# Two masked-attention layers: one count per group, and projections in halves in the counts' bank

## The chip, the cores and the metric

One core of one Trainium2 chip runs the whole program. The metric is the device time of one launch in microseconds; three runs of the kernel before gave a median of 3095.62 (3095.62 to 3095.9).

## The reference

There are 16 graphs ("batches") of N = 1024 nodes with E = 256 features, in float32, and a 0/1 adjacency matrix of 1024 x 1024 for each. Each batch goes through two layers. A layer normalizes the features of each node, applies a relu, projects to queries, keys and values, computes attention scores only where the adjacency says so, and adds the projected result to its input.

```python
for layer, (H, D) in enumerate([(4, 64), (8, 32)]):
    h = maximum(layernorm(x), 0)
    q, k, v = h @ Wq, h @ Wk, h @ Wv            # layer 1 has biases
    s = q @ k.T / sqrt(D)                       # per head: 1024 x 1024
    s = where(adj > 0, s, -inf)
    x = x + softmax(s) @ v @ Wo + bo
```

The softmax divides each head's weighted sum of values by the sum of its exponentials. That sum of exponentials over the keys is what this kernel calls a count.

## The kernel before

**Tiling.** For each batch and layer the queries are split into two halves of 512 (`qh`), and the heads into two groups (`g`) that fill 128 partitions: 2 heads of 64 in layer 0, 4 heads of 32 in layer 1. So a layer of a batch has four groups; in the order (qh, g) they are called group 0 to group 3 here. A group is made of steps: 4 in layer 0, 8 in layer 1. In a step, `scores` (L493) computes four blocks of 128 keys x 512 queries on TensorE into two pairs of PSUM banks; `exponentials` (L508) masks each pair on VectorE (L524) into a tile `p` in SBUF and applies the exponential on ScalarE (L530); `weigh` (L535) multiplies the result with the values on TensorE (L542), two steps behind the scores. Layer 0 of batch b + 2 and layer 1 of batch b + 1 follow layer 1 of batch b, so that a batch's two layers never run back to back: the list of 768 steps is L0 of batch 0, then L0 of batch b + 1 and L1 of batch b by turns. One turn is 16 steps of layer 0 (run two at a time) and 32 steps of layer 1.

**PSUM.** Six of the eight banks are three pairs (`ps_s`) used in a ring by the scores, and by projections, transposes and output products in between. The two other banks (`ps_o`) hold one tile each: `po` for the weighted values and `pz` for the counts.

**SBUF ring of the exponentials.** The tile of an even step is one of 7 (`p0`); an odd step takes two half tiles, each one of 2 (`p10`, `p11`). So the odd tile of step s is written again by step s + 4, once its reader on GpSimd (POOL) is through.

**Counting in layer 1.** A count is a matmul of `p` with ones (`count`, L381): TensorE sums over 128 keys. To need few of them, tiles are added first. `count_steps` (L645) does it: behind each odd step, POOL adds the odd step's two half tiles into the even step's tile (L659, two instructions). Four such pairs make a group. Pairs are then joined by a DMA that adds one tile to another (`accumulate`, L642, issued on POOL, 1 MiB each): in groups 0 to 2 the first pair into the second, and the third into the fourth. So two tiles are left, each counted by 4 matmuls of 512 columns (each of which the hardware runs as two) or, in two following steps, by halves of 256 columns (`halves`, L689). In group 3 the first two and the third are accumulated on, and one tile is counted. The last group of batch 14 (`brief`) and all of layer 1 of batch 15 (`pairs`) count without this chain.

**After a group.** `end_group` (L700) gives the steps in which the count is copied out (`spread`), inverted (`invert`), read back in broadcast form (`fetch`), multiplied into the result on POOL (`normalize`), and, once per query half, multiplied by Wo and added to x (`end_half`, L478, 16 matmuls).

**Inputs of later layers.** While layer 1 of batch b runs, the inputs of layer 0 of batch b + 2 are prepared (`other`), and those of layer 1 of batch b + 1 (`mine` in the next turn of the loop over b): `stats` on VectorE and POOL, `norm` on ScalarE, then transposition by blocks through DRAM (`turn_blocks` on VectorE, `put_blocks` and `place_blocks` by DMAs on SyncE's queue, tile names `hn` and `turned`), then `k`, `q` (8 matmuls of 512 each) and `values` (16 matmuls of 256), each into a pair of PSUM banks, copied out by ScalarE or VectorE.

**Order.** The program writes its order out by hand. `later(i, f, ...)` puts a piece of work into step i; `Stream.run` (L588) emits for each step: scores; then the weighing that is due (in an even step of layer 1 with a piece of `LARGE` work it waits for the odd step that follows); then the counts that are due; then masking and exponentials; then the other pieces, the large ones last. A DMA that POOL issues stands in POOL's own instruction order: if it has to wait, what follows on POOL waits too.

The steps given to the pieces are offsets: `c` is the first step of layer 1 of batch b, and `a` = c - 16 the first step of the layer 0 (of batch b + 1) that stands ahead of it; a - 22 to a - 1 lie in layer 1 of batch b - 1. In `end_group` the offsets count from the step in which a group's last weighing is due, two behind the group's last step.

Of the kernel before, what the change touches and what calls it, by code (L numbers as in the profile page):

```python
# [18 lines left out]
P = 128  # L19
# [4 lines left out]

LARGE = ("k", "q", "values", "end_half")
COUNTS = ("count", "count_added")
# [64 lines left out]
def fast_program(ctx, tc, a, w, loads, chk):  # L91
# [89 lines left out]
    class Inputs:  # L181
# [98 lines left out]
        def place_blocks(self, half):  # L280
# [3 lines left out]
            for k in range(4):  # L284
                nc.sync.dma_start(
                    hT[ts(k, 32)].rearrange("p c (g q) -> p c g q", q=P), blocks[k]
                )

        def kq(self, half, is_q):
            if half == 0 and not is_q:  # L290
                self.kT = actp.tile([P, 2, N], F32, tag="kT", name=f"kT_{self.n}")
                self.v = actp.tile([P, NT, E], F32, tag="v", name=f"v_{self.n}")
            if is_q:
# [31 lines left out]
        def test(self):  # L325

            held = small.tile([P, 32], F32, tag="held", bufs=1, name=f"held_{self.n}")
            for i in range(self.sums.shape[1] // 32):
                for bound, op in ((SUM_MIN, ALU.is_ge), (SUM_MAX, ALU.is_le)):
# [3 lines left out]
                    nc.gpsimd.tensor_mul(chk, chk, held)  # L333

        def k(self, half):
            self.kq(half, False)
# [231 lines left out]
    class Stream:  # L568
# [76 lines left out]
        def count_steps(self, i, st):  # L645
# [7 lines left out]
            elif j % 2:  # L653
# [6 lines left out]
                if gr.pairs and (st.last or gr.hurry):  # L660
                    self.later(i + 2, gr.count, one, j == 1, st.last)
                elif gr.pairs:
                    self.halves(i + 3, gr, one, j == 1, False)
                elif j == 1:
                    gr.one = one
                elif j == 3:
                    self.accumulate(one, gr.one)
                    gr.one = one
                    if not gr.last:
                        self.halves(i + gr.waits[0], gr, one, True, False)  # L670
                    if gr.brief:
                        self.later(i + 6, gr.count, one, True, False)
                elif gr.brief and j == 5:
                    self.halves(i + 5, gr, one, False, False)
                elif gr.brief:
                    self.later(i + 4, gr.count, one, False, st.last)
                elif j == 5:
                    gr.two = one
# [21 lines left out]
        def end_group(self, i, gr):  # L700
# [6 lines left out]
            if gr.layer == 0:  # L707
# [121 lines left out]
    def block_inputs(inp, half, turn, put, place, *at):  # L829

        later(turn, inp.turn_blocks, half)
        later(put, inp.put_blocks, half)
        later(place, inp.place_blocks, half)
        for i, f in zip(at, (inp.k, inp.q, inp.values)):
            later(i, f, half)

# [18 lines left out]
    for b in range(B - 1):  # L855
# [7 lines left out]
        else:  # L863
            norms(mine, 0, a - 20, a - 16, a - 15, a - 13, bias=a)
            block_inputs(mine, 0, a - 10, a - 8, a - 4, a, a + 2, a + 8)
            norms(mine, 1, a - 14, a - 10, a - 8, a - 6, bias=a + 6)
            block_inputs(mine, 1, a, a + 6, a + 7, c, c + (6 if b + 2 < B else 10), c + 2)
        for i, u in zip((0, 2, 4, 6, 7, 9, 11, 13), range(NT)):
            later(a + i, masks[b].second, u)
        if b + 2 < B:  # L870
# [3 lines left out]
            if b == 0:  # L874
                norms(other, 0, a + 12, a + 14, c, c + 1, bias=c + 34)
                block_inputs(other, 0, c + 2, c + 3, c + 4, c + 8, c + 16, c + 18)
                norms(other, 1, c + 3, c + 4, c + 6, c + 7, bias=c + 36)
                block_inputs(other, 1, c + 8, c + 9, c + 12, c + 22, c + 26, c + 30)
# [267 lines left out]
```

## Time and profile before

| | |
|---|---|
| median of 3 runs | 3095.62 us |
| the profiled execution | 3096.61 us, of it 3094.8 from the first to the last instruction |
| granted TensorE clock | 0.999 |
| TensorE matmuls busy | 3074.0 us (99%) |
| VectorE, ScalarE, GpSimd busy | 2474.6 (80%), 2230.1 (72%), 2436.5 (79%) |
| one layer 0 in the middle (batch 7) | 76.8 us |
| one layer 1 in the middle (batch 5) | 113.1 us |

The page gives for each group of instructions its line, engine, operation and tiles, how often it ran, the time it was busy, the mean of one, and how long its engine was idle just before it and for whom. A timeline row gives the start, the time to the end of the last of the merged instructions, and in brackets the idle time before it. A "landing" is the time at which a DMA has signalled that its data is written, counted from its issue.

### The profile page before, as it was taken

Reading aid. Unit: us, or ns where it says so; the run is one execution under the profiler, and the core shown is the slowest. Engines: PE = TensorE matmul, PEld = TensorE weight load, DVE = VectorE, ACT = ScalarE, POOL = GpSimd, SP = SyncE. Lnnn points to the kernel's source line nnn. Section 1 sums busy time; section 2 is a strip of 40 time slices with the busy share of each in tenths; the row PEclk is TensorE's granted clock in tenths of the full one; section 3 lists DMA queues with packets and bytes.
Section 4 is the critical chain, followed back from the end, with each engine's and each line's share of the span. In section 5 each row is a group of like instructions: output and inputs, shape, how many; then the busy total and the mean of one; then the engine's idle time right before and its main releaser. Section 6 shows DMA issues by size and latency. Waiting matters only on the chain.

```text
span 3094.8 us, 47328 instructions
## 1 busy us (share of the span) xinstructions
PE 3074.0 (99%) x17406; PEld 1221.3 (39%) x17406; DVE 2474.6 (80%) x2698; ACT 2230.1 (72%) x2436; POOL 2436.5 (79%) x1554
## 2 busy tenths in 40 slices
PE   9999999999999999999999999999999999999998
PEld 4443433434334343343434334343343433434333
DVE  6778788887888878788787888878788787887777
ACT  5677777777777777778677677776777777776676
POOL 3578878787887878878788787887878778787787
PEclk9999999999999999999999999999999999999999
DMA  5215545454463544635445353554535545453331
GB/s 129 66 58 118 127 106 129 121 112 119 107 137 110 119 118 103 143 108 117 120 103 134 107 127 110 113 127 110 127 110 111 132 105 125 120 112 84 79 77 33
DMA packets 259230, 341.37 MB, mean 110 GB/s; under 512 B 58288, under 2 KB 218288, under 8 KB 241968
## 3 DMA queue, kind: packets, MB, share of 16 engines
q0 software_dynamic: 19152, 139.47, 22.6%
q1 hardware_dynamic: 238368, 197.51, 22.2%
q8 instruction: 138, 2.26, 0.3%
q10 hardware_dynamic: 1472, 1.31, 0.2%
q14 instruction: 100, 0.82, 0.1%
HBM read 149.95 MB, written 47.96 MB: 64 GB/s over the span
## 4 chain that ended last, share of the span: by engine, by line
PE 95%; DVE 2%; POOL 1%; DMA 1%; issue 1%; ACT 0%; SPq 0%; DVEq 0%; ACTq 0%; POOLq 0%
PE ps L501 31%; PE po L542 29%; PE pq L304 15%; PE pv L345 8%; PE py L483 7%; PE pz L387 4%; DVE p L524 1%; POOL p L659 1%; DMA inv<-vd 0%; DMA x<-in_x_dram 0%; SPq L420 0%; ACT p L530 0%; DMA sums<-s 0%; POOL cat L447 0%; DMA adj<-in_adj_dram 0%
## 5 line engine op out<-in xcount | busy, mean ns | idle before, releaser
L524 DVE SCALAR_TENSOR_TENSOR p<-mask,ps 128x1024 f32<-128x1024 fp8e5 x1536 | 1791.9, 1214 | 366.2 <-PE ps L501 348.5
L530 ACT ACTIVATE p<-p 128x1024 f32<-128x1024 f32 x1536 | 1607.0, 1056 | 628.1 <-DVE p L524 572.1
L659 POOL TENSOR_TENSOR p<-p,p 128x1024 f32<-128x1024 f32 x510 | 1212.8, 2430 | 166.3 <-PE po L542 165.8
L501 PE MATMUL ps<-qT,kT 32*128 32x512 f32 (+1 forms) x6144 | 1073.3, 628 | 3.6 <-DVE p L524 3.0
L542 PE MATMUL po<-p,v 128*32 128x512 f32 (+1 forms) x6144 | 980.2, 600 | 0.7 <-ACT cat L399 0.4
L501 PEld LDWEIGHTS ps<-qT,kT 32*128 32x128 f32 (+1 forms) x6144 | 349.7, 184 | 587.9 <-issue 243.1
L542 PEld LDWEIGHTS po<-p,v 128*32 128x32 f32 (+1 forms) x6144 | 234.3, 118 | 680.3 <-issue 474.5
L555 POOL TENSOR_TENSOR p<-p 128x1024 f32<-128x1024 f32 x128 | 302.7, 2365 | 90.5 <-DVE p L554 85.1
L554 POOL TENSOR_TENSOR p<-p,p 128x1024 f32<-128x1024 f32 x64 | 150.8, 2356 | 169.6 <-DVE p L551 126.3
L345 PE MATMUL pv<-wv,hT 128*128 128x256 f32 x1024 | 237.8, 385 | 0.0
L304 PE MATMUL pq<-hT,wk 128*128 128x512 f32 x512 | 236.7, 605 | 0.7 <-DVE p L524 0.6
L304 PE MATMUL pq<-hT,wq 128*128 128x512 f32 x512 | 236.6, 605 | 0.1
L483 PE MATMUL py<-wo,cat 128*128 128x256 f32 x1008 | 234.4, 386 | 0.7 <-DVE p L524 0.6
L447 POOL TENSOR_TENSOR cat<-cat,inv 128x512 f32<-128x512 f32 x127 | 174.9, 1383 | 73.0 <-DMA inv<-vd 72.6
L345 PEld LDWEIGHTS pv<-wv,hT 128*128 128x128 f32 x1024 | 189.4, 190 | 72.1 <-DVE p L524 21.3
L483 PEld LDWEIGHTS py<-wo,cat 128*128 128x128 f32 x1008 | 186.3, 190 | 74.8 <-issue 25.1
L551 DVE TENSOR_TENSOR p<-p 128x1024 f32<-128x1024 f32 x128 | 181.7, 1419 | 0.0
L387 PE MATMUL pz<-p,ones 128*32 128x256 f32 (+1 forms) x1928 | 180.4, 444 | 0.5 <-DMA p<-p 0.5
L643 POOL DMA_DIRECT2D p<-p x133 | 122.6, 922 | 63.7 <-POOL p L659 30.3
L221 ACT ACTIVATE hn<-x,shift,rstd 128x256 f32<-128x256 f32 x251 | 135.6, 588 | 43.7 <-DMA turned<-hn 32.2
L399 ACT COPY cat<-po 128x512 f32<-128x512 f32 x128 | 73.4, 573 | 118.5 <-PE py L483 96.6
L488 DVE TENSOR_TENSOR x<-py,x 128x1024 f32<-128x1024 f32 x63 | 77.1, 1224 | 101.9 <-PE py L483 101.2
(62 smaller groups left out, 1773.1 us busy)
## 6 DMA issues: line engine op xcount, KB each, us to landing
p<-p POOLq DMA_DIRECT2D x133, 1024.0 KB, 7.8
adj<-in_adj_dram SPq DMA_DIRECT2D x504, 128.0 KB, 3.0
turned<-hn SPq DMA_DIRECT2D x58, 512.0 KB, 3.8
hT<-turned SPq DMA_DIRECT2D x232, 128.0 KB, 2.8
x<-in_x_dram SPq DMA_DIRECT2D x128, 128.0 KB, 3.1
inv<-vd SPq DMA_DIRECT2D x128, 128.0 KB, 3.0
inv<-vd SPq DMA_DIRECT2D x252, 64.0 KB, 3.3
out_dram<-x SPq DMA_DIRECT2D x124, 128.0 KB, 2.3
```

Source lines behind the costliest of these rows:

```text
L304: nc.tensor.matmul(pq[:, m, :], wt[self.layer][:, c, ts(m, P)], self.hT[half][:, c, :], start=(c == 0), stop=(c == 1),)
L345: nc.tensor.matmul(pv[:, i, :], self.hT[half][:, c, ts(i, P)], w.v[self.layer][:, c, :], start=(c == 0), stop=(c == 1),)
L387: nc.tensor.matmul(self.s[ts(r, 32), q], w.ones.to_broadcast([P, 32]), of[:, q], start=start and not part, stop=stop and part != 0,)
L447: nc.gpsimd.tensor_mul(o, o, inv)
L483: nc.tensor.matmul(py[:, i, :], self.half.cat[:, c, ts(i, P)], w.o[self.layer][:, c, :], start=(c == 0), stop=(c == 1),)
L501: nc.tensor.matmul(st.ps[i // 2][:, i % 2, :], gr.inp.kT[r * D : (r + 1) * D, gr.g, ts(kt, P)], gr.inp.qT[gr.qh][r * D : (r + 1) * D, gr.g ...
L524: nc.vector.scalar_tensor_tensor(out=half, in0=gr.mask.m[gr.qh][:, kt // 4, :, kt % 4].unsqueeze(1).to_broadcast([P, 2, 512]), scalar=-EDG ...
L530: nc.scalar.activation(half, half, AF.Exp, scale=gr.scale)
L542: nc.tensor.matmul(gr.o[r * D : (r + 1) * D, :], gr.inp.v[:, kt, h * D : (h + 1) * D], st.halves[i // 2][:, i % 2, :], start=(kt == 0), st ...
L551: nc.vector.tensor_add(a, a, b)
L555: nc.gpsimd.tensor_add(a, a, b)
L659: nc.gpsimd.tensor_add(half, half, of)
```

## The change

In layer 1 of batches 0 to 14, groups 0 to 2 now accumulate all four pairs into one tile, which is counted once: the first pair into the second, the second into the third in the same step as that pair's adds, and the third into the fourth two steps behind the adds (`self.later(i + k, self.accumulate, ...)`, k = 2). The count stands 9, 7 and 8 steps behind the end of group 0, 1 and 2, in one piece except in group 1. Group 3 is as it was.

Two thirds of the projections for layer 0 of batches 2 to 15 are made in two parts, each with one half of the output, in the bank `pz` of the counts (`part`, `k_part`, `q_part`, `values_part`), and the parts stand in different steps. Keys: steps c + 8 and c + 10 for half 0, c + 20 and c + 22 for half 1. Queries: c + 12 and c + 16 for half 0. Values: c + 28 and c + 30 for half 1.

Some pieces move: for layer 0's second query half the normalization from 7 to 11 and the product from 11 to 13 steps behind its end (steps c + 12 and c + 14); the copy and inverse of groups 0 and 2 of layer 1; the statistics for the next layer 1 by two or three steps earlier.

```diff
-LARGE = ("k", "q", "values", "end_half")
+LARGE = ("k", "q", "values", "end_half", "k_part", "q_part", "values_part")
...
+        def part(self, half, is_q, m):
+            if m == 0 and is_q:
+                self.qT[half] = actp.tile(
+                    [P, 2, 512], F32, tag="qT", bufs=3, name=f"qT_{self.n}_{half}"
+                )
+            to = self.qT[half] if is_q else self.kT[:, :, ts(half, 512)]
+            wt = w.q if is_q else w.k
+            pq = ps_o.tile([P, 512], F32, tag="pz", name=f"pq_{self.n}_{half}_{int(is_q)}_{m}")
+            for c in range(2):
+                nc.tensor.matmul(
+                    pq, wt[self.layer][:, c, ts(m, P)], self.hT[half][:, c, :],
+                    start=(c == 0), stop=(c == 1),
+                )
+            (nc.vector.tensor_copy if is_q else nc.scalar.copy)(to[:, m, :], pq)
...
+        def values_part(self, half, m):
+            pv = ps_o.tile([P, 512], F32, tag="pz", name=f"pv_{self.n}_{half}_{m}")
+            pv = pv.rearrange("p (t e) -> p t e", e=E)
+            for i in range(2):
+                for c in range(2):
+                    nc.tensor.matmul(
+                        pv[:, i, :], self.hT[half][:, c, ts(2 * m + i, P)],
+                        w.v[self.layer][:, c, :], start=(c == 0), stop=(c == 1),
+                    )
+            nc.scalar.copy(self.v[:, 4 * half + 2 * m : 4 * half + 2 * m + 2, :], pv)
...
-            self.waits = ((5, 5), (7, 7), (7, 6), None)[2 * qh + g]
+            self.waits = (9, 7, 8, 4)[2 * qh + g]
...
-                elif j == 3:
+                elif gr.brief:
+                    if j == 3:
+                        self.accumulate(one, gr.one)
+                        self.later(i + 6, gr.count, one, True, False)
+                    elif j == 5:
+                        self.halves(i + 5, gr, one, False, False)
+                    else:
+                        self.later(i + 4, gr.count, one, False, True)
+                elif gr.last and j == 5:
+                    gr.two = one
+                elif not st.last:
                     self.accumulate(one, gr.one)
                     gr.one = one
-                    if not gr.last:
-                        self.halves(i + gr.waits[0], gr, one, True, False)
...
-                elif not gr.last:
-                    self.accumulate(one, gr.two)
-                    if gr.qh:
-                        self.later(i + 6, gr.count, one, False, True)
+                else:
+                    of, k = (gr.two, 1) if gr.last else (gr.one, 2)
+                    self.later(i + k, self.accumulate, one, of)
+                    if gr.g and not gr.qh:
+                        self.halves(i + gr.waits, gr, one, True, True)
                     else:
-                        self.halves(i + gr.waits[1], gr, one, False, True)
-                else:
-                    self.later(i + 1, self.accumulate, one, gr.two)
-                    self.later(i + 4, gr.count, one, True, True)
+                        self.later(i + gr.waits, gr.count, one, True, True)
...
-                at = (3, 4, 5, 7, 11) if gr.qh else (3, 5, 6, 7, 11)
+                at = (3, 4, 5, 11, 13) if gr.qh else (3, 5, 6, 7, 11)
...
-                at = ((6, 12, 15, 19), (8, 12, 14, 17, 19), (6, 9, 11, 14), None)[2 * gr.qh + gr.g]
+                at = ((9, 13, 15, 19), (8, 12, 14, 17, 19), (8, 11, 13, 15), None)[2 * gr.qh + gr.g]
...
-            norms(mine, 0, a - 20, a - 16, a - 15, a - 13, bias=a)
+            norms(mine, 0, a - 22, a - 18, a - 15, a - 13, bias=a)
...
-            norms(mine, 1, a - 14, a - 10, a - 8, a - 6, bias=a + 6)
+            norms(mine, 1, a - 14, a - 13, a - 8, a - 6, bias=a + 6)
...
-                block_inputs(other, 0, c, c + 1, c + 2, c + 8, c + 16, c + 18)
+                block_inputs(other, 0, c, c + 1, c + 2, (c + 8, c + 10), (c + 12, c + 16), c + 18)
...
-                block_inputs(other, 1, c + 7, c + 8, c + 12, c + 22, c + 26, c + 30)
+                block_inputs(other, 1, c + 7, c + 8, c + 12, (c + 20, c + 22), c + 26, (c + 28, c + 30))
```

More of the change, by code (lines that the diff above doesn't have):

```diff
@@ L287, in place_blocks, with open_kv @@
                 )
+        def open_kv(self):
+            self.kT = actp.tile([P, 2, N], F32, tag="kT", name=f"kT_{self.n}")
+            self.v = actp.tile([P, NT, E], F32, tag="v", name=f"v_{self.n}")
         def kq(self, half, is_q):
             if half == 0 and not is_q:
-                self.kT = actp.tile([P, 2, N], F32, tag="kT", name=f"kT_{self.n}")
-                self.v = actp.tile([P, NT, E], F32, tag="v", name=f"v_{self.n}")
+                self.open_kv()
             if is_q:
@@ L333, in test, with k_part, q_part @@
                     nc.gpsimd.tensor_mul(chk, chk, held)
+        def part(self, half, is_q, m):
[12 more added lines that the diff above has]
+            (nc.vector.tensor_copy if is_q else nc.scalar.copy)(to[:, m, :], pq)
+        def k_part(self, half, m):
+            if half == 0 and m == 0:
+                self.open_kv()
+            self.part(half, False, m)
+        def q_part(self, half, m):
+            self.part(half, True, m)
+        def values_part(self, half, m):
[8 more added lines that the diff above has]
+            nc.scalar.copy(self.v[:, 4 * half + 2 * m : 4 * half + 2 * m + 2, :], pv)
         def k(self, half):
@@ L665, in count_steps @@
                     gr.one = one
-                elif j == 3:
+                elif gr.brief:
[9 more added lines that the diff above has]
+                elif not st.last:
                     self.accumulate(one, gr.one)
                     gr.one = one
-                    if not gr.last:
-                        self.halves(i + gr.waits[0], gr, one, True, False)
[L671 to L678, printed above, removed]
-                elif not gr.last:
-                    self.accumulate(one, gr.two)
-                    if gr.qh:
-                        self.later(i + 6, gr.count, one, False, True)
-                    else:
-                        self.halves(i + gr.waits[1], gr, one, False, True)
-                else:
-                    self.later(i + 1, self.accumulate, one, gr.two)
-                    self.later(i + 4, gr.count, one, True, True)
+                else:
[3 more added lines that the diff above has]
+                        self.halves(i + gr.waits, gr, one, True, True)
+                    else:
+                        self.later(i + gr.waits, gr.count, one, True, True)
         def halves(self, i, gr, one, start, stop):
@@ L833, in block_inputs @@
         later(place, inp.place_blocks, half)
-        for i, f in zip(at, (inp.k, inp.q, inp.values)):
-            later(i, f, half)
+        parts = inp.k_part, inp.q_part, inp.values_part
+        for i, f, part in zip(at, (inp.k, inp.q, inp.values), parts):
+            if type(i) is tuple:
+                for m in range(2):
+                    later(i[m], part, half, m)
+            else:
+                later(i, f, half)
     for i, f, half in (0, inp.k, 1), (0, inp.values, 0), (0, inp.values, 1), (2, inp.q, 1):
@@ L875, in fast_program @@
                 norms(other, 0, a + 12, a + 14, c, c + 1, bias=c + 34)
[L876 removed]
+                block_inputs(other, 0, c + 2, c + 3, c + 4, (c + 8, c + 10), (c + 12, c + 16), c + 18)
                 norms(other, 1, c + 3, c + 4, c + 6, c + 7, bias=c + 36)
[L878 removed]
+                block_inputs(other, 1, c + 8, c + 9, c + 12, (c + 20, c + 22), c + 26, (c + 28, c + 30))
             else:
                 norms(other, 0, a + 10, a + 12, a + 13, a + 15, bias=c + 34)
[L881 removed]
+                block_inputs(other, 0, c, c + 1, c + 2, (c + 8, c + 10), (c + 12, c + 16), c + 18)
                 norms(other, 1, c + 2, c + 4, c + 5, c + 6, bias=c + 36)
[L883 removed]
+                block_inputs(other, 1, c + 7, c + 8, c + 12, (c + 20, c + 22), c + 26, (c + 28, c + 30))
             at = 5, 8, 10, 12, 14, 45, 49, 51, 53
```

## The prediction

> **What bounds the kernel now.** I read the page first, then the groups with shapes kept apart, then the timelines of TensorE and GpSimd in one batch, then the DMA view of two short windows.
>
> ```profile
> PE 3074.0 (99%) x17406; PEld 1221.3 (39%) x17406; DVE 2474.6 (80%) x2698; ACT 2230.1 (72%) x2436; POOL 2436.5 (79%) x1554
> L659 POOL TENSOR_TENSOR p<-p,p 128x1024 f32<-128x1024 f32 x510 | 1212.8, 2430 | 166.3 <-PE po L542 165.8
> L387 PE MATMUL pz<-p,ones 128*32 128x256 f32 (+1 forms) x1928 | 180.4, 444 | 0.5 <-DMA p<-p 0.5
> L643 POOL DMA_DIRECT2D p<-p x133 | 122.6, 922 | 63.7 <-POOL p L659 30.3
> ```
>
> TensorE is idle for 21 us in all, so a matmul taken out pays at once, as long as nobody else becomes late. The candidate is POOL: in layer 1 of batch 5 (span 1149.80 to 1262.90) the windows view has it busy 94.60 of 113.10 us. All times below count from that 1149.80, and step n is the n-th step from there; other batches differ by tenths. Here is POOL from step 18 on:
>
> ```profile
> 1223.28 9.39 POOL L659 TENSOR_TENSOR p<-p,p 128x1024 f32<-128x1024 f32 x4 [1.75 <-PE po L542]
> 1232.96 0.87 POOL L643 DMA_DIRECT2D p<-p  x1 [0.30 <-POOL p L659]
> ...
> 1248.69 4.72 POOL L659 TENSOR_TENSOR p<-p,p 128x1024 f32<-128x1024 f32 x2 [1.64 <-PE po L542]
> 1253.37 1.28 POOL L447 TENSOR_TENSOR cat<-cat,inv 128x512 f32<-128x512 f32 x1
> 1254.62 4.71 POOL L659 TENSOR_TENSOR p<-p,p 128x1024 f32<-128x1024 f32 x2
> 1259.62 0.89 POOL L643 DMA_DIRECT2D p<-p  x1 [0.30 <-POOL p L659]
> 1261.42 4.70 POOL L659 TENSOR_TENSOR p<-p,p 128x1024 f32<-128x1024 f32 x2 [0.90 <-PE po L542]
> 1267.91 0.87 POOL L643 DMA_DIRECT2D p<-p  x1 [1.79 <-PE po L542]
> ```
>
> Two things to see. POOL waits for TensorE before each pair of adds, by 0.4 to 2.2 us: that is all its slack. And the last row: the accumulate at 1267.91 reads the tile that the one of 1259.62 writes. That one lands at 1267.37 (issue plus 7.7), and POOL starts 0.54 later; in all 14 batches with this pair the second starts 0.5 to 0.6 us after the first has landed. So the wait put down to PE is one for the landing, and it stops everything behind it on POOL. Landings depend on company; the DMA view of 1212:1227 and then of 1231:1246:
>
> ```profile
> p<-p POOLq DMA_DIRECT2D x1, 1024.0 KB, 6.9
> ```
>
> ```profile
> p<-p POOLq DMA_DIRECT2D x1, 1024.0 KB, 10.0
> turned<-hn SPq DMA_DIRECT2D x1, 512.0 KB, 9.6
> inv<-vd SPq DMA_DIRECT2D x4, 64.0 KB, 7.5
> ```
>
> At step 22 the accumulate meets the block write and the read-backs: 10.0 to 11.8 us there, median 10.1, in 14 of 14 batches.
>
> **What TensorE saves.** From one start to the next in the trace, a half count (8 matmuls of 256) takes 0.55 us and a full one (8 of 512) 0.98. Before, groups 0 and 1 have four halves each (2.2), group 2 two halves and a full one (2.1). After: 0.98, 1.1, 0.98. That is 1.2 + 1.1 + 1.1 = 3.4 us a batch, in batches 0 to 14: 51 us at most. The projections cost the same in halves: a whole one holds TensorE 3.64 us, a half 1.82. They fill the pairs of steps that lose their counts (10, 14, 20, 28), which matters because a bare pair is 4.0 us on TensorE against 4.86 us of masking on VectorE and 4.7 of adds on POOL; every pair now has at least 5.1.
>
> **What it adds off TensorE.** 45 accumulates (three in groups 0 to 2, not two): 0.3 + 0.61 us of POOL each. Two copies of 512 for one of 1024: ScalarE 2 x 0.586 for 1.005, VectorE 2 x 0.69 for 1.224, four times a batch, some 0.7 us on engines with over 15 us free in that stage. The parts leave the score buffers alone and share the bank of the counts instead; the closest case is the k half of step 22, whose copy (behind that step's exponentials) ends near 83.7 while the count in step 24 starts at 86.6. If that cover went, 1 us per case would show. Layer 0's normalization (two of 1.25) leaves step 8, behind the new second accumulate of group 0, for step 12: POOL reaches step 13's adds at 52.5 for 50.2, and is level again by step 19. SP issues group 0's four read-outs in step 18 instead of 15 and its inverse in 22 instead of 21, with the same block write and read-backs behind them; it waits for others most of the time there, so nothing. ScalarE stands for the block write before the norm of step 24 (2.1 us in this batch); it gets there 2.2 us earlier and the write does not, so the exponentials of step 25 end near 96.4, just when TensorE wants them in step 27: between nothing and 1 us, and I take nothing, because the later event below covers it.
>
> **The wait that is added.** A1, A2 and A3 are a group's accumulates in order. A2 (behind the third pair's adds) reads what A1 wrote one pair of adds before. In groups 0 and 1 a whole product lies between (pair 7.64 us): wait under 1 us. In group 2 it is a half (5.85). I follow the chain from step 19, which TensorE reaches at 71.18 - 2.18 (four half counts gone) + 0.98 (group 0's count, now in step 18) = 69.98, plus 0.2 since layer 0's products in step 14 now come right behind their normalization on POOL (moved to step 12, behind group 0's A3).
> - Adds start 2.3 behind the step (as in the trace): 72.5; 4.69; statistics moved here from step 22, 1.58; A3 of group 1 at 79.1; adds from 79.7; A1 of group 2 at 84.7.
> - It lands 10.1 later (write and read-backs stand at the same place), 94.8. POOL is through with its adds at 90.3 and stands until A2 at 95.35. Behind it: adds for two pairs, 95.95 to 105.3; A3; a normalization of 1.25; adds to 112.2.
> - A1 of group 3 goes out at 112.5; before, 109.8. It lands 7.9 later (median of this place), 120.4; then 0.54, and the 11.1 us that lie between the same two accumulates before (1267.91 to 1279.03): the final one at 132.1. It lands 8.5 later: 140.6.
> - The count of group 3 stands behind that landing on TensorE. Before, it started at 140.43 (1290.23) with the data there since 137.1. After, TensorE alone would be there at 140.4 - 3.4 = 137.0.
>
> So the saving is used up before that count: 140.6 against 140.4. On the way the pair of adds of step 25 is 6.4 us late (95.95 for 89.5), so VectorE gets its odd buffer for step 27 4 us late; the three score pairs cover some 2 us, and TensorE stands for the rest. With the 0.2, and 0.7 for steps 31 to 33, TensorE's own arrival is 139.9 at least, so the later of the two decides in many batches: I take +0.5 a batch. Fourteen batches: +7. Batch 14's last group counts without that final accumulate, so part of its 3.4 stays: -2. The profiled execution took 3096.61 (span 3094.8): 3101.6; the median runs lie 1.0 below it: 3101.
>
> One rule speaks against counting matmuls at all. The row: PE busy 99%, with the start-to-start times above. The Trainium skill, Perfetto Trace Analysis, Identifying the Most-Contended Engine, says that matmul busy time misjudges TensorE's headroom and that weight-load busy time should be read, here 39%; by it no matmul time would come back, and even the 51 us offered would be nothing. I go by the row.
>
> A second one concerns the landing. The row: an accumulate keeps the 16 engines 5.26 us (22.6% of 3094.8 over 133) and lands in 6.8 at the least. The Trainium skill, DMA: Bandwidth & Descriptors, Specifications, gives 435 GB/s as the ceiling; 1 MiB would move in an estimated 2.4 us, A2 would never wait, and the time would be near 3045. The measured rows decide.
>
> **Rivals.** (1) Faster: A1 of group 2 lands like its sisters, in about 7. Then A2 goes at 92.2, the chain ends at 137.5, VectorE is late by 0.9, which the buffers cover, and 2.9 to 3.4 us a batch stay: -41 - 3, 3052; at a landing of 8.5, 3072. For it: 6.8 to 7.0 is the usual landing; against it: the write has its place still, and A3 of group 1 now comes 5.6 us ahead. (2) Slower: this A3 and A1 run in one software queue, with 5.26 us of engine time each, and the write and read-backs between them (some 3.2, from 21.6% of 15 us). If A1 is held up 2 us more (12.1), every batch gets 2.2 longer: +31, 3126. From a landing of about 9.9 on, the batch is longer than before; the row's worst is 11.8.
>
> **How the numbers follow.** My case (the landings take the saving, 3087 to 3112): 0.48. Rival 1: 0.30. Rival 2: 0.22. About 0.2% (6.2 us) is what a measurement tells from no change. Faster is rival 1 and 0.07 of my case, 0.37; same 0.20; slower 0.43. The unknowns are landings: 6.9 to 12.1 at one place gives 3052 to 3126, which is the range.
>
> **What would show it.** Right: 178 accumulates; POOL's accumulate rows waiting for p<-p some 4 to 5 us once a batch at step 23; counts waiting for DMA p<-p; PE idle up by 40 to 60 us while the pz row falls from 180 to about 130; the layer 1 stage shorter and the count of group 3 still near 140 after its start. Wrong: landings near 7 at step 24, PE still 99% busy, a period near 186.

## The result, and the profile after

The changed kernel took 3127.74 us (median of 4 runs, 3126.51 to 3131.29) against 3095.76 (4 runs, 3095.62 to 3096.21) for the kernel before: a ratio of 1.0099, 95% interval 1.0086 to 1.0112. The forecast was 3101 with a range of 3052 to 3126: the sign of its largest chance held, the size did not, and the time lies 1.7 us outside the range. The profiled execution of the changed kernel took 3131.3 us, 3128.7 of it span; against 3094.8 before that is 33.9 us more to explain. One run each of experiments 1, 3 and 11 was far longer than the others (6089, 3474 and 7391 us); the medians given there count it, which moves them by 1 us at most, and the ratios leave it out.

Line numbers have moved: masking is now L562 (L524 before), VectorE's first add in layer 0 L589 (L551), POOL's pair adds L697 (L659), the accumulates L681 (L643), the counts L425 (L387). The page of the changed kernel: engines, the chain of work that ended last by engine, and the groups of the accumulates and VectorE's add.

```profile
PE 3076.9 (98%) x16566; PEld 1202.3 (38%) x16566; DVE 2527.9 (81%) x2712; ACT 2236.2 (71%) x2478; POOL 2470.4 (79%) x1599
PE 68%; POOL 13%; DMA 8%; DVE 5%; issue 3%; ACT 2%; SPq 1%; POOLq 0%; ACTq 0%; DVEq 0%
L681 POOL DMA_DIRECT2D p<-p x178 | 167.9, 943 | 176.8 <-DMA p<-p 98.7
L589 DVE TENSOR_TENSOR p<-p 128x1024 f32<-128x1024 f32 x128 | 235.8, 1842 | 0.0
```

The chain and VectorE's add before:

```profile
PE 95%; DVE 2%; POOL 1%; DMA 1%; issue 1%; ACT 0%; SPq 0%; DVEq 0%; ACTq 0%; POOLq 0%
L551 DVE TENSOR_TENSOR p<-p 128x1024 f32<-128x1024 f32 x128 | 181.7, 1419 | 0.0
```

TensorE has 840 matmuls fewer and stands idle for 51.8 us instead of 20.8. The chain was 95% TensorE before; now POOL, DMAs and VectorE hold 26% of it. Before its accumulates POOL is idle for 176.8 us instead of 63.7. And VectorE's add takes 1842 ns on average where it took 1419: nothing in the change touches it.

POOL from step 18 of batch 5 on, the rows that answer to those of before (this layer 1 starts at 1157.96):

```profile
1237.05 0.91 POOL L681 DMA_DIRECT2D p<-p  x1
1237.71 4.99 POOL L697 TENSOR_TENSOR p<-p,p 128x1024 f32<-128x1024 f32 x2
1242.99 0.87 POOL L681 DMA_DIRECT2D p<-p  x1 [0.30 <-POOL p L697]
1243.60 5.02 POOL L697 TENSOR_TENSOR p<-p,p 128x1024 f32<-128x1024 f32 x2
1253.71 0.86 POOL L681 DMA_DIRECT2D p<-p  x1 [5.09 <-PE pq L307]
1254.32 9.61 POOL L697 TENSOR_TENSOR p<-p,p 128x1024 f32<-128x1024 f32 x4
...
1271.01 0.87 POOL L681 DMA_DIRECT2D p<-p  x1 [0.30 <-POOL p L697]
...
1279.91 0.88 POOL L681 DMA_DIRECT2D p<-p  x1 [3.30 <-DMA p<-p]
1280.52 5.00 POOL L697 TENSOR_TENSOR p<-p,p 128x1024 f32<-128x1024 f32 x2
1285.17 4.98 POOL L230 TENSOR_TENSOR x<-x,bo 128x1024 f32<-128x1024 f32 x2
1289.81 1.56 POOL L485 TENSOR_TENSOR cat<-cat,inv 128x512 f32<-128x512 f32 x1
1291.02 1.19 POOL L681 DMA_DIRECT2D p<-p  x1
```

The predicted chain is there: A3 of group 1 at 79.1, A1 of group 2 at 85.0, A2 at 95.75 behind a stand of 5.09 us (the row names TensorE, which had long been done; A1 landed 0.5 earlier), A1 of group 3 at 113.05, the final accumulate at 133.1. The DMA view of 1242:1253 has the landing that A2 waited for:

```profile
p<-p POOLq DMA_DIRECT2D x1, 1024.0 KB, 10.2
turned<-hn SPq DMA_DIRECT2D x1, 512.0 KB, 3.5
inv<-vd SPq DMA_DIRECT2D x4, 64.0 KB, 7.5
```

But the count of group 3 started at 141.97 after the start, without a wait: the data had landed 0.3 us before. TensorE itself came that late, not at the predicted 139.9. What made VectorE, and by it TensorE, late is in the list of waits, here of the changed kernel and then of before (total us, times, longest):

```profile
POOL p L681 <- DMA p<-p: 98.7, 29, 4.9
DVE p L562 <- POOL p L697: 93.4, 103, 2.6
```

```profile
POOL p L643 <- DMA p<-p: 14.9, 7, 3.5
DVE p L524 <- POOL p L659: 4.5, 6, 1.1
```

The waits of masking for an odd buffer that POOL still reads went from 4.5 to 93.4 us. One row of VectorE's timeline, in step 35:

```profile
1286.73 5.73 DVE L589 TENSOR_TENSOR p<-p 128x1024 f32<-128x1024 f32 x1
```

This add takes 1.22 us when it is left alone; the one in the same step before took 2.55:

```profile
1277.91 2.55 DVE L551 TENSOR_TENSOR p<-p 128x1024 f32<-128x1024 f32 x1
```

Here it ends at 1292.46, which is 1.09 us after the last tensor instruction of POOL's unbroken run (the normalization, over at 1289.81 + 1.56 = 1291.37): nearly its own length. The issue of the accumulate that ends the run, over at 1292.21, does not hold it.

That TensorE came almost together with the data is no coincidence. In all 14 batches with this chain the count of group 3 starts 7.47 to 7.55 us after the end of this add (8.04 to 10.38 before) and 0.14 to 0.41 us after the landing (0.91 to 3.76 before). Both follow from the end of the same POOL run. In experiments 6 and 9, where the add is short, count and landing part again, by 1.0 and 2.8 us on average.

The table below is used for all experiments: the mean over batches 1 to 12 of the time from one step's first score matmul to another's, counted from the start of layer 1 (steps 0 to 32 are layer 1, 32 to 48 the next layer 0), from each kernel's trace. The last column is layer 1 of batch 14 and all that follows it. The rows from e1_no_a1 on stand in the order of experiments 1 to 12.

| steps | 0-16 | 16-24 | 24-28 | 28-32 | 32-34 | 34-36 | 36-38 | 38-48 | sum | batches 14, 15 |
|---|---|---|---|---|---|---|---|---|---|---|
| before | 58.76 | 28.08 | 12.73 | 13.71 | 9.12 | 10.85 | 11.99 | 44.54 | 189.78 | 236.8 |
| changed | 59.26 | 26.45 | 13.35 | 13.68 | 10.01 | 11.81 | 12.43 | 44.56 | 191.55 | 244.8 |
| e1_no_a1 | 59.19 | 26.55 | 12.75 | 11.84 | 9.98 | 10.85 | 12.10 | 44.71 | 187.96 | 248.3 |
| e2_write_early | 59.27 | 26.92 | 12.89 | 11.93 | 9.98 | 11.28 | 12.76 | 44.55 | 189.57 | 245.0 |
| e3_group2_back | 59.01 | 26.55 | 13.26 | 13.59 | 9.12 | 10.85 | 11.99 | 44.58 | 188.95 | 239.1 |
| e4_a2_late | 59.25 | 26.45 | 13.36 | 11.84 | 9.12 | 14.96 | 12.05 | 44.91 | 191.96 | 241.3 |
| e6_a2_late_a3_early | 59.19 | 26.45 | 13.37 | 11.84 | 9.99 | 11.57 | 13.21 | 44.94 | 190.56 | 242.2 |
| e11_adds_ahead | 59.45 | 26.45 | 13.38 | 11.84 | 10.03 | 11.62 | 11.99 | 44.50 | 189.25 | 243.5 |
| e5_wholes | 59.32 | 29.30 | 12.82 | 13.65 | 9.98 | 10.85 | 12.22 | 44.73 | 192.84 | 245.3 |
| e7_batch14_back | 59.13 | 26.45 | 13.38 | 14.01 | 10.01 | 11.58 | 12.27 | 44.84 | 191.66 | 237.0 |
| e8_bias_late | 59.59 | 26.45 | 13.38 | 13.91 | 10.01 | 11.66 | 11.99 | 45.97 | 192.94 | 243.6 |
| e9_all_three | 59.59 | 26.45 | 13.37 | 11.84 | 10.01 | 11.60 | 11.99 | 46.17 | 191.03 | 237.6 |
| e12_group2_alone | 60.18 | 28.49 | 12.71 | 11.88 | 9.99 | 11.10 | 12.15 | 44.93 | 191.43 | 237.2 |
| e10_group2_batch14_back | 59.02 | 26.55 | 13.26 | 13.59 | 9.12 | 10.85 | 11.99 | 44.58 | 188.94 | 237.1 |

The first two rows divide the 33.9 us: 13 periods took 24.0 more (2490.8 for 2466.8), batches 14 and 15 8.0, the start up to the first layer 1 1.3, the period of batch 0 0.5.

### The profile page after: what moved, and what is told of

The parts are those of the page before. It is cut to its first block, busy times and chain, and to the rows that moved or that the text cites. A ratio compares the mean times of both kernels' runs of the same rounds, so it can differ in the third digit from the quotient of the medians.

```text
span 3128.7 us, 45854 instructions
## 1 busy us (share of the span) xinstructions
PE 3076.9 (98%) x16566; PEld 1202.3 (38%) x16566; DVE 2527.9 (81%) x2712; ACT 2236.2 (71%) x2478; POOL 2470.4 (79%) x1599
## 4 chain that ended last, share of the span: by engine, by line
PE 68%; POOL 13%; DMA 8%; DVE 5%; issue 3%; ACT 2%; SPq 1%; POOLq 0%; ACTq 0%; DVEq 0%
PE ps L539 22%; PE po L580 21%; POOL p L697 11%; PE py L521 7%; PE pq L307 6%; PE pv L383 6%; DMA p<-p 5%; PE pq L348 3%; PE pz L425 2%; DVE p L562 2%; DMA vd<-vn 2%; DVE p L589 1%; POOL cat L485 1%; PE pv L367 1%; POOL rstd L211 0%
## 5 line engine op out<-in xcount | busy, mean ns | idle before, releaser
L562 DVE SCALAR_TENSOR_TENSOR p<-mask,ps 128x1024 f32<-128x1024 fp8e5 x1536 | 1794.9, 1213 | 392.6 <-PE ps L539 270.7
L697 POOL TENSOR_TENSOR p<-p,p 128x1024 f32<-128x1024 f32 x510 | 1242.7, 2571 | 86.6 <-PE po L580 86.4
L539 PE MATMUL ps<-qT,kT 32*128 32x512 f32 (+1 forms) x6144 | 1110.5, 629 | 22.2 <-ACT kT L324 9.7
L681 POOL DMA_DIRECT2D p<-p x178 | 167.9, 943 | 176.8 <-DMA p<-p 98.7
L589 DVE TENSOR_TENSOR p<-p 128x1024 f32<-128x1024 f32 x128 | 235.8, 1842 | 0.0
L592 POOL TENSOR_TENSOR p<-p,p 128x1024 f32<-128x1024 f32 x64 | 150.9, 2359 | 105.5 <-DVE p L589 87.8
L307 PE MATMUL pq<-hT,wq 128*128 128x512 f32 x400 | 184.8, 605 | 8.0 <-DVE p L562 8.0
L383 PE MATMUL pv<-wv,hT 128*128 128x256 f32 x800 | 185.7, 385 | 1.1 <-DVE p L562 1.1
L383 PEld LDWEIGHTS pv<-wv,hT 128*128 128x128 f32 x800 | 148.0, 190 | 58.2 <-DVE p L562 13.6
L167 ACT ACTIVATE mask<-adj,numbers 128x1024 fp8e5<-128x1024 int32 x128 | 145.5, 1139 | 22.3 <-DMA adj<-in_adj_dram 22.3
L595 POOL TENSOR_TENSOR p<-p,p 128x1024 f32<-128x1024 f32 x64 | 152.1, 2376 | 5.0
L230 POOL TENSOR_TENSOR x<-x,bo 128x1024 f32<-128x1024 f32 x64 | 155.9, 2509 | 0.0
L178 ACT ACTIVATE mask<-mask,numbers 128x1024 fp8e5<-128x1024 fp8e5 x128 | 144.2, 1136 | 0.0
```

The costliest lines, as they stand in the source:

```text
L307: nc.tensor.matmul(pq[:, m, :], wt[self.layer][:, c, ts(m, P)], self.hT[half][:, c, :], start=(c == 0), stop=(c == 1),)
L383: nc.tensor.matmul(pv[:, i, :], self.hT[half][:, c, ts(i, P)], w.v[self.layer][:, c, :], start=(c == 0), stop=(c == 1),)
L539: nc.tensor.matmul(st.ps[i // 2][:, i % 2, :], gr.inp.kT[r * D : (r + 1) * D, gr.g, ts(kt, P)], gr.inp.qT[gr.qh][r * D : (r + 1) * D, gr.g ...
L562: nc.vector.scalar_tensor_tensor(out=half, in0=gr.mask.m[gr.qh][:, kt // 4, :, kt % 4].unsqueeze(1).to_broadcast([P, 2, 512]), scalar=-EDG ...
L589: nc.vector.tensor_add(a, a, b)
L681: nc.gpsimd.dma_start(one, two, accum_op=ALU.add)
```

## Experiments

All ran in three groups beside the kernel before on the same chip; a ratio is to that kernel, with its 95% interval. Its medians were 3098.6, 3098.1 and 3097.8 us there, 2 to 3 us above the 3095.76 beside the changed kernel, so a difference of an experiment's time to 3127.74 is not sure to better than that.

**1. Is it group 2's first accumulate?** In batches 0 to 13 its first pair is joined to nothing and left out of the count:

```diff
                 elif not st.last:
-                    self.accumulate(one, gr.one)
+                    if not (gr.qh and not gr.g and j == 3 and gr.inp.b < B - 2):
+                        self.accumulate(one, gr.one)
                     gr.one = one
```

> The changed kernel without the first accumulate of group 2 in batches 0 to 13 (its first pair is left out of the count); the second one then waits for no landing. Theory (POOL stands for that landing, the odd tile buffers come free late, TensorE stands for scores): POOL reaches the adds of step 25 some 5 us earlier, the 4 us of standing per batch between steps 26 and 36 go, 14 x 4 = 56 off 3127.7: 3065 to 3080. Rival A (the half projections in the counts' bank are what costs): only 14 accumulates of 0.9 us of POOL less, 3115 to 3128. Rival B (45 more accumulates load DMA engines and POOL in general): 14 of 45 less, a third of 32 us: 3113 to 3120.

Measured: 3082.46 us, ratio 0.9942 (0.9922 to 0.9962). Without that one wait of POOL, and with 14 accumulates of 178 fewer, the kernel is faster than before; both rivals, from 3113 on, are out. Steps 28 to 32 fall to 11.84 us, and 34 to 36 to 10.85. The waits of masking for odd buffers fall from 93.4 to 25.3 us.

**2. Company of the landing.** The block write for the next layer 1 (and the transposition ahead of it) comes one to three steps earlier, group 0's read-backs two later:

```diff
-                at = ((9, 13, 15, 19), (8, 12, 14, 17, 19), (8, 11, 13, 15), None)[2 * gr.qh + gr.g]
+                at = ((9, 13, 17, 19), (8, 12, 14, 17, 19), (8, 11, 13, 15), None)[2 * gr.qh + gr.g]
...
-            block_inputs(mine, 0, a - 10, a - 8, a - 4, a, a + 2, a + 8)
+            block_inputs(mine, 0, a - 12, a - 11, a - 4, a, a + 2, a + 8)
```

> The changed kernel with the block transposition and its write to DRAM in steps 20 and 21 instead of 22 and 24, and group 0's read-backs two steps later, so that group 2's first accumulate has no company. Theory (the landing at this one place decides): it lands in 7 to 8 instead of 10.2, POOL stands some 2 us instead of 5, TensorE's standing falls from 4 to about 1 a batch: 3080 to 3092. Rival A (half projections) and rival B (number of accumulates): the same work in all, 3122 to 3130.

Measured: 3099.33 us, ratio 1.0005 (0.9995 to 1.0014). Its POOL timeline, at A1 and A2 of group 2:

```profile
1234.89 0.87 POOL L681 DMA_DIRECT2D p<-p  x1 [0.30 <-POOL p L697]
...
1242.92 0.87 POOL L681 DMA_DIRECT2D p<-p  x1 [2.40 <-DMA p<-p]
```

The landing falls to about 7.5 us with A3 of group 1 still ahead, the stand from 5.09 to 2.40, and 28 us of the 32 come back. So it is the company of the write and read-backs that makes 10.2 of 7.5, not the accumulate ahead. The expected 3080 to 3092 is missed by 7 us: steps 34 to 38 stay 1.2 us longer than before. Something else is late there.

**3. Undo group 2.** It is counted in two parts as before, the others as changed:

```diff
+                elif gr.qh and not gr.g and j == 3:
+                    self.accumulate(one, gr.one)
+                    self.halves(i + 7, gr, one, True, False)
+                elif gr.qh and not gr.g and j == 5:
+                    gr.two = one
+                elif gr.qh and not gr.g:
+                    self.accumulate(one, gr.two)
+                    self.later(i + 6, gr.count, one, False, True)
                 elif not st.last:
```

Its copy and inverse go back to (6, 9, 11, 14), the second half's values to one piece in step 30.

> The changed kernel with group 2 counted twice as before (two accumulates, half counts in steps 28 and 29, a full one in step 31) and the values of half 1 whole in step 30; groups 0 and 1 stay counted once. Theory: no second accumulate waits beside the block write, TensorE does 1.1 us more per batch and stands 4 less: 3127.7 - 14 x 2.9 = 3087, 3080 to 3092, so faster than before. Rival A (half projections): 6 of 8 parts are left, so 3118 to 3126. Rival B: 30 of 45 accumulates left, 3113 to 3120.

Measured: 3087.1 us, ratio 0.9959 (0.9943 to 0.9975): faster than both kernels. From step 32 on every stretch is that of before. What is left of the change brings 0.83 us a batch.

**4. Move group 2's accumulates.** A2 two steps later (`self.later(i + 2, self.accumulate, one, gr.one)`); then A3 must come later, in step 29, the count in step 35, and its copy and inverse behind it.

> The changed kernel with all its accumulates and one count per group, but group 2's second accumulate two steps later (behind the next pair's adds), its third one two steps later, its count in step 35 instead of 33 and the copy and inverse after it. Theory: the landing is waited for behind 4.7 us of adds, so POOL hardly stands; TensorE's 4 us a batch go: 3068 to 3082. Rival A and rival B: the same parts and the same accumulates, 3122 to 3130.

Measured: 3121.47 us, ratio 1.0063 (1.0046 to 1.008): a miss. Steps 28 to 32 are freed (11.84), but steps 34 to 36 take 14.96:

```profile
1283.06 1.77 POOL L681 DMA_DIRECT2D p<-p  x2 [0.30 <-POOL p L697]
```

A3 and the A1 of group 3 now leave back to back. In batches 0 to 13 the first lands 7.3 to 9.0 us after its issue and the second 12.1 to 13.5. That is the queueing of two accumulates that the second rival spoke of, at a place where I had put it myself. But group 2's count does not stand for it: in batch 5 it starts 9.8 us after the later landing. What stands is in the list of waits:

```profile
ACT mask L167 <- DMA adj<-in_adj_dram: 47.4, 15, 3.7
PE ps L539 <- ACT kT L324: 26.1, 9, 3.7
```

In batches 1 to 7 the last adjacency load issued beside the two accumulates lands 12 us after its issue (the median of all such loads in the changed kernel is 3.0). ScalarE waits for it for 2.7 to 3.5 us ahead of its copy of the keys for the next layer 1, and TensorE stands 2.7 to 3.5 us in step 35 for these keys. The granted clock in step 35 was 0.78 to 0.86 in batches 2 to 7 and 1.00 in the others, which makes this step another 1.6 to 2.7 us longer in the six; the count that is now in it costs 1.0. That the accumulates hold up these loads is read from the trace and was not tested by itself. The profiled execution, from which the row of the table comes, is the slowest of the four, 3132.19 us.

**5. The same with A3 earlier.** A3 in step 28 and the count in step 33 (k = 3 for group 2).

> The changed kernel with group 2's second accumulate two steps later and its third in step 28 (it was step 29 in the run before, together with group 3's first, where it landed 12 to 13 us after its issue and the count stood for it); the count is back in step 33. Theory (what counts is the time POOL stands and when the tile has landed): the third lands near 113, the count comes near 115, steps 26 to 32 take 20 us instead of 21.9 and nothing new stands: 188 a batch instead of 191.6, 3072 to 3086. Rival (two accumulates close together are the cost wherever they stand): 3110 to 3130.

Measured: 3112.02 us, ratio 1.0043 (1.0026 to 1.006): above the theory's 3086 and inside the rival's range. Half of the loss is gone. Part of what is left stands in this POOL timeline:

```profile
1263.87 0.87 POOL L681 DMA_DIRECT2D p<-p  x1 [0.30 <-POOL p L697]
...
1273.97 0.87 POOL L681 DMA_DIRECT2D p<-p  x1 [4.48 <-PE pq L307]
```

Group 3's A1 leaves 5.9 us behind A3 and lands 9.6 us after its issue. Its second accumulate, which reads that tile, makes POOL stand for 4.48 us, ahead of the adds of the last pair.

**6. Those adds ahead of that wait.** On top of experiment 5, one order changed:

```diff
-                if gr.last and not (gr.brief or gr.pairs) and j == 7:
-                    self.accumulate(gr.two, gr.one)
                 for k, of in enumerate(st.halves):
                     half = one[:, ts(k, 2), :]
                     nc.gpsimd.tensor_add(half, half, of)
+                if gr.last and not (gr.brief or gr.pairs) and j == 7:
+                    self.accumulate(gr.two, gr.one)
```

> e6_a2_late_a3_early with one order changed: group 3's accumulate of its second pair onto its first is issued behind the adds of its last pair, not ahead of them. Theory: in e6 POOL stood 4.5 us at step 33 for the landing of the accumulate before, with the last pair's adds queued behind it, so the odd buffers came free late (steps 34 to 36 took 11.6 us, not 10.85). With the adds ahead POOL works through that landing: steps 34 to 36 10.8 to 11.0 us, steps 36 to 38 12.0 to 13.2, so 0.7 to 1.9 us less in each of 13 batches than e6: 3086 to 3103 us. Rival: VectorE's add of step 35 is what makes 34 to 38 long, and it stays at over 5 us because POOL runs without a break; then steps 36 to 38 stay at 13.2 and the time is within 5 us of e6, 3107 to 3117.

Measured: 3093.38 us, ratio 0.9986 (0.9976 to 0.9995): 18.6 us below experiment 5. POOL and then VectorE at the same place:

```profile
1257.10 9.64 POOL L695 TENSOR_TENSOR p<-p,p 128x1024 f32<-128x1024 f32 x4
1266.57 1.00 POOL L681 DMA_DIRECT2D p<-p  x1
1267.18 5.13 POOL L230 TENSOR_TENSOR x<-x,bo 128x1024 f32<-128x1024 f32 x2
1275.37 1.26 POOL L485 TENSOR_TENSOR cat<-cat,inv 128x512 f32<-128x512 f32 x1 [3.06 <-DMA inv<-vd]
```

```profile
1272.67 1.22 DVE L589 TENSOR_TENSOR p<-p 128x1024 f32<-128x1024 f32 x1
```

POOL does four adds in a row through the landing, so its bias adds are over at 1272.31, before VectorE's add begins, and that add is back at 1.22 us (1.54 on average over batches 1 to 12, against 5.77 in experiment 5). The gain came from there (36 to 38: 13.21 to 11.99), not from 34 to 36 as expected, where 11.57 stayed 11.62. The rival, that the add stays long, is out, and so is that of experiment 5: the two accumulates are as close as there, and 18.6 us came back.

**7. The halves of the projections.** Whole again, with the new counts: `c + 8, c + 16, c + 18` and `c + 22, c + 26, c + 30`.

> The counts of the changed kernel with layer 1's projections whole again (keys at step 8, queries at 16, values at 18 and 30, keys at 22 of layer 1, one pair of banks each). Theory: a half took 1.92 us and a whole 3.64, so eight halves give back 8 x 0.1 = 0.8 us in each of 14 batches and nothing else moves: 3114 to 3120 us, ratio 1.006 to 1.008. Rival 1: a whole projection takes one of the two pairs of banks that the scores use, so the scores behind it stand for its copy and the halves were worth having: 3128 to 3145 us. Rival 2: TensorE's time is not what steps 24 to 38 wait for, so nothing moves: 3125 to 3130.

Measured: 3151.15 us, ratio 1.0171 (1.0154 to 1.0188). The halves are worth 23 us. The first rival had the sign, with a range that ends 6 us too low, but not the whole reason: the long wait of projections for score buffers is no longer than before (61.6 us there, 63.5 here):

```profile
PEld pq L307 <- DVE p L562: 63.5, 75, 2.0
```

```profile
PEld pq L304 <- DVE p L524: 61.6, 75, 1.5
```

What grew is the pair with neither count nor projection. Steps 20 to 24 hold one whole (3.63) and two pairs of steps (4.0 each), 11.63 us, and took 13.03; with two halves (3.84) they took 11.90, almost their sum. In batch 5 TensorE stood 1.0 us at the scores of the bare pair of steps 20 and 21 and 0.27 at those of step 22, as the prediction's 4.86 us of masking against 4.0 says of such pairs.

**8. Batch 14.** Groups 0 to 2 of batch 14 counted in two parts as before.

> The changed kernel with batch 14's groups 0 to 2 counted twice as before (that batch has no projections of a later layer 0 between its steps). Theory: there POOL is the bound and every stand for a landing goes through to TensorE; layer 1 of batches 14 and 15 take 237 us as before instead of 245: 3117 to 3121. Rival (the tail is longer for what the earlier batches leave behind): 3126 to 3130.

Measured: 3121.51 us, ratio 1.0074 (1.0057 to 1.009). Batches 14 and 15 together fall from 244.8 to 237.0 us: the 8 us belong to the new counts of batch 14. POOL stood there 2.0, 4.5 and 2.7 us for landings.

**9. The bias adds.** Four adds of POOL (L230) moved from steps 32 to 38 to steps 42 to 49, so that VectorE's add of step 35 has no run of POOL beside it.

> The changed kernel with POOL's four bias additions of a batch (2.34 us each) moved from steps 32 to 38 to steps 42 to 49, where POOL had gaps. Theory (POOL's unbroken run up to step 36 also holds up VectorE's add of step 35, 5.7 us instead of 1.2, and so TensorE in steps 34 to 38): 1.4 us a batch come back, the 4 us of steps 26 to 30 stay: 3104 to 3112; the add of step 35 takes under 2.5 us. Rival (the saving ends at the landing of group 3's last accumulate): that accumulate goes out 4.7 us earlier, so all that it held back returns, 3090 to 3100; or POOL's order there decides nothing: 3126 to 3130.

Measured: 3149.78 us, ratio 1.0171 (1.0154 to 1.0188): a miss. The add of step 35 fell to 1.22 us and 36 to 38 to 11.99, but 34 to 36 kept 11.66, and the adds that were moved lengthened 38 to 48 by 1.4 us. VectorE's adds there run beside them and wait in their turn: in step 47 one took 1.84 us on average, 1.16 in the changed kernel.

**10. Experiments 5, 8 and 9 in one.**

> The three edits together: group 2's later accumulates, batch 14 counted as before, the bias additions in later steps. Theory: the parts add up, 3127.7 - 48 - 9 - 18 = 3053, 3048 to 3062, with TensorE standing under 0.5 us a batch: under both kernels. Rival (POOL's total work is the bound once its stands are gone): no lower than the sum without one of them, 3070 to 3085.

Measured: 3111.11 us, ratio 1.0045 (1.0031 to 1.0059): a miss, above the rival's range too. One of the three edits alone costs 22 us (experiment 9), and with that the measured parts add up to 3128; the three together are 17 us below that, so they do not simply add. Steps 38 to 48 cost 1.6 us again, and POOL's stand for group 3's A1 was still there.

**11. Group 2 alone.** Groups 0 and 1, batch 14 and most projections as before; group 2 in one count.

> The other half of e3_group2_back: of layer 1's counts only group 2's (batches 0 to 13) and group 3's steps are as in the changed kernel; groups 0 and 1, batch 14 and the projections are as before, except that the values of the second half stay in two parts. Theory: group 2's single count, with its two accumulates on POOL ahead of group 3's, carries the whole loss, and the others bring 0.8 us a batch: the changed kernel's period less e3's is 2.6 us, so before's 189.8 + 2.6 = 192.4 us, 3096 + 14 x 2.6 = 3132 us (3122 to 3140), ratio 1.009 to 1.014. Rival: the loss needs the accumulates of groups 0 and 1 and the halves as well (they put POOL and the queue behind before group 2 starts); then it is 3096 to 3115.

Measured: 3123.09 us, ratio 1.0078 (1.0057 to 1.0098). The time is in the expected range, but not for the expected reason. From step 16 to 38 the mean is 86.3 us, against 86.5 before and 87.7 in the changed kernel: there group 2's single count costs nothing on balance. The loss stands in steps 0 to 16 (+1.4, all of it in steps 12 to 15), where layer 0's normalization and product have their changed place beside group 0's old counts, a mix that neither kernel has; which of the two it is was not tested. So the theory that group 2 carries the loss by itself falls in this form. The stand at A2 is smaller, but there:

```profile
1256.94 0.88 POOL L681 DMA_DIRECT2D p<-p  x1 [2.47 <-PE ps L539]
```

From the start of layer 1 (1161.9) A2 leaves at 95.0 in this batch, at 98.0 and 96.0 in batches 3 and 9, hardly otherwise than the changed kernel's 95.8; but TensorE reaches step 24 only at 88.7 (the first two columns), not at 85.7. The chain of accumulates looks like a floor: step 38 is reached at 146.5 us here and at 147.0 in the changed kernel, whether groups 0 and 1 have been counted once or twice ahead of it. In experiment 3 it lies lower (final accumulate at 128.8 on average; 132.5 here, 133.4 in the changed kernel), step 38 comes at 144.4, and what groups 0 and 1 save is kept. That the floor is the same in this mix is read from the traces and was not tested by itself.

**12. The two undoings that paid.** Experiments 3 and 8 in one kernel.

> Two undoings at once, in the changed kernel: group 2 counted in two parts as before in all batches (as in e3_group2_back), and groups 0 to 2 of batch 14 counted in two parts as before (as in e7_batch14_back). Theory: the two losses stand in different batches and add up. e3's layer-1 stretches of batches 14 and 15 took 113.9 + 125.2 = 239.1 us against the 237.0 of e7, so some 2 us below e3: 3083 to 3087 us, ratio to before 0.995 to 0.9965, mean layer-1 period of batches 1 to 12 at e3's 188.95, batches 14 and 15 together 236.5 to 237.5. Rival: most of what batches 14 and 15 lost came from group 2's accumulates alone, which e3 has taken back already; then batches 14 and 15 stay at 239 and the time at e3's 3086 to 3089.

Measured: 3084.45 us, ratio 0.9959 (0.9945 to 0.9973), the fastest kernel here that counts everything: 43 us below the changed kernel. Time, period (188.94) and batches 14 and 15 (237.1 us) lie where the theory put them; from experiment 3 it is only some 2 us away. Its page:

```profile
PE 3053.2 (99%) x16846; PEld 1203.4 (39%) x16846; DVE 2470.9 (80%) x2712; ACT 2239.0 (73%) x2464; POOL 2461.8 (80%) x1582
```

TensorE's busy time is 20.8 us below before, its idle time 28.9 instead of 20.8, and the difference is the 12.7 us that the span lost.

## Why the prediction was right or wrong

**Right: the chain of accumulates.** Against batch 5: A1 of group 2 issued at 84.7 (85.0), landed 94.8 (95.2), A2 at 95.35 (95.75), A1 of group 3 at 112.5 (113.05), the final one at 132.1 (133.1), landed at 140.6 (141.7). The stand of 5 us at A2 and the late odd buffers behind it were named; experiments 1 to 3, which take away the wait, its company or the second accumulate, confirm them as the main cost.

**Wrong: TensorE's own arrival, 139.9.** That was the step that failed: the text let the landing decide, with an arrival that was "at least" 139.9, and took +0.5 us a batch. It was 141.97. Worked out anew: 140.4 before, less 3.4 of counts, plus 0.8, 4.0 and 0.2, is 142.0.
- The 0.8: a half projection holds TensorE for 1.92 us, not 1.82; there are eight. "The projections cost the same" was wrong by that.
- The 4.0: TensorE stood 0.5, 1.78 and 0.44 us at steps 26, 28 and 29, where some 2.0 was priced, and 0.95 and 0.37 at steps 34 and 36, where 0.7 was taken for this part (at steps 31 to 33). The prediction saw neither cause of this second pair.

The 0.95 is a stand for the keys of the next layer 1, in each of the 14 batches; before the change no matmul waited for them:

```profile
PE ps L539 <- ACT kT L324: 9.7, 14, 0.7
```

ScalarE's copy of them ends 2.63 us after the start of step 34, 1.48 before (means of batches 1 to 12). Ahead of it stand exponentials whose masking waited for an odd buffer that POOL still read: 1.76 us in steps 30 to 34, nothing before and in experiment 3. The copy of group 2's count, which the change put there, does not explain it: experiments 1 and 7 have it ahead of the keys as well, with these waits at 0.27 and 0.15 us, and take 10.85 us for steps 34 to 36. POOL's stand of 3.30 us for group 3's A1 and the long add are not the cause either, since experiment 6, nearly without both, and experiment 9, without the long add, keep 11.6. The 0.37 is VectorE's add, held for as long as POOL's run lasts (5.73 us, 2.55 before): where it is short, in experiments 6 and 9, steps 36 to 38 are back at 11.99.

A period is so 1.77 us longer, not 0.5: 24 us in 13 of them. Of the signs that the prediction named, the 178 accumulates and the stand at A2 came; the count of group 3 waited for no landing, and TensorE's idle time grew by 31 us, not by 40 to 60.

**Wrong: batch 14.** It was put at -2 and was +8 with batch 15 (experiment 8). The prediction looked only at the end of its chain, the missing final accumulate, and not at the landing waits ahead of it, which stop POOL for 9.3 us in that layer (2.04, 4.52 and 2.72).

**The rivals.** The second one, slower by 31, came within 2 us of the time, and that was luck: the landing was 10.2 us, not 12.1. Two accumulates do hold each other up when they leave back to back, as experiment 4 shows, but 6 us apart they need not: in experiment 2, A1 of group 2 lands in 7.5 us with A3 of group 1 that far ahead. The first did occur in experiment 2: a landing of 7.5 us, for which it gave between 3052 and 3072. The measured 3099 shows that it, too, was priced with the landing alone.

**Right in part: what counts save and what halves fill.** Experiment 3 has groups 0 and 1 with one count each and is 0.83 us a batch below before, of the 2.3 that their counts were priced at; six halves take 0.6 of the difference, and the rest was not followed up. In experiment 12 the TensorE time came back in the span: at 99% busy, taking out 20.8 us of matmuls gave 12.7 us. That the halves fill the pairs which lose their counts was worth 23 us (experiment 7).

## What to carry to other kernels

Where an engine issues DMAs in its own order, count the time from the issue to the landing against the work that lies between, and put work that somebody waits for ahead of an issue that has to wait. When a change lets two chains of waits reach an engine in one stage, work out that engine's own arrival with every stand in it, and not only the time of the data; where two arrivals agree to tenths of a microsecond in every batch, look for what both hang on. A conversion that pays in one place need not pay in the next: here undoing one of three turned a loss into a gain.

## What the runs showed of the hardware that was not expected

VectorE's add of two SBUF tiles does not share with POOL's adds: it stands until POOL's run has a gap. In the changed kernel 33 of these 192 adds (L589, L592) began inside a POOL instruction of over 2 us (0.1 us or more behind its start and 0.3 or more ahead of its end), and all 33 were long, over 1.4 and up to 5.8 us; of the other 159, 154 took under 1.4 us. All that took over 1.4 us, 26 before, 38 in the changed kernel and 22 in experiment 3, end 1.08 or 1.09 us after the end of a tensor instruction of POOL, nearly the 1.22 us that one takes alone; the issue of an accumulate behind that instruction does not hold them. Where the add came first, POOL waited: a POOL instruction of 0.20 us that started beside it took 1.27 in step 45. Masking, which reads PSUM and SBUF, ran at 1.21 us beside the same POOL adds. Over the span the time above 1.22 us an add comes to 32 us of VectorE before, 83 in the changed kernel and 13 in experiment 6.

The Trainium skill, SBUF — State Buffer, section "SBUF: two separate sides", has the rule for it: a VectorE operation with two inputs in SBUF and a GpSimd operation that reads SBUF exclude one another, and whichever starts first keeps the ports for the whole instruction. The traces agree, and add that the one that waits stays blocked over several POOL instructions in a row (three in the 5.73 us), not for one.

In batches 0 to 13 of the kernel before, where no two accumulates were on their way together, one of 1 MiB landed in 6.8 to 9.6 us after its issue, and in 10.0 to 11.8 beside the block write and the read-backs. With another 5.9 us ahead it was 7.5 in experiment 2 and 9.6 in experiment 5; what made that difference was not tested. Of two that left back to back in experiment 4, the first landed in 7.3 to 9.0 us and the second in 12.1 to 13.5.
